# A conditioned transformer block on one core: layer-norm statistics shared between two engines, turned tokens kept by half, and some instructions moved in their queues

## The chip, the core and the metric

The kernel runs on one core of a Trainium2 chip. The core has TensorE (PE in the profile, with its weight loads listed apart as PEld), VectorE (DVE), ScalarE (ACT), GpSimd (POOL) and SyncE (SP), which issues most DMAs. Each engine works through its own queue in the order in which the program was written; engines wait for one another by semaphores. Matmuls write to PSUM, the small memory of banks beside the large on-chip SBUF.

The metric is device time in microseconds. A time given for a kernel is the median of its runs; the profile is of one execution, whose own time is given beside it.

## The reference, cut to what matters

```python
emb = jnp.dot(jax.nn.silu(t), ada_w) + ada_b            # adaLN, six parts of 512
shift_msa, scale_msa, gate_msa, shift_mlp, scale_mlp, gate_mlp = jnp.split(emb, 6, axis=-1)
norm = _ln(x) * (1.0 + scale_msa[:, None]) + shift_msa[:, None]
h = jax.nn.gelu(jnp.dot(norm, ssm_w1) + ssm_b1, approximate=False)
x = x + gate_msa[:, None] * (jnp.dot(h, ssm_w2) + ssm_b2)
norm2 = _ln(x) * (1.0 + scale_mlp[:, None]) + shift_mlp[:, None]
hf = jax.nn.gelu(jnp.dot(norm2, ff_w1) + ff_b1, approximate=True)
x = x + gate_mlp[:, None] * (jnp.dot(hf, ff_w2) + ff_b2)
```

x is 2 x 2048 x 512 in fp32 and t is 2 x 512. `_ln` subtracts the mean over the 512 features and divides by the root of the variance plus 1e-6. The weights are 512 x 3072 (ada_w), 512 x 512 (ssm_w1, ssm_w2), 512 x 1024 (ff_w1) and 1024 x 512 (ff_w2), all fp32.

## The kernel before

The 4096 tokens are cut into 8 blocks of 512. A block lies in SBUF as 128 partitions x 4 slots (c = 0 to 3) x 512 features. A block passes through: statistics (mean and variance of each token, `mv`), root (`ve`, and `r` by a power on GpSimd), a few tiny VectorE steps to `rstd` and `nmr`, `normal(c)` on ScalarE, a turn of tokens against features, the modulation by adaLN's shift and scale, the layer `hA` (W1 and GELU), the layer `oA` (W2, residual), a second norm, and the layers `hC` and `oC` of the feed-forward part.

All matrix products are made by fast recursive schemes: a product is split into quarters, and seven half-size products (P1 to P7) are made of sums of quarters in place of eight. So beside the matmuls there are sums of operands: of weights (`w1_sums`, `fw1_sums`, on GpSimd at L386), of tokens (`summed`, also recorded at L386, on VectorE or GpSimd) and of hidden values (`hSA`). `hidden` and `residual` issue the products of one layer in the order given (`FIRST` is P1, P2, P5, P6, P7, P3, P4; block 0's first layer runs P1, P2, P5, P6, P3, P7, P4). After each product VectorE reads its PSUM bank, ScalarE applies GELU where it is due, and then the hooks of that product run.

The order of all other work is written out by hand: `hook(hooks, ("P2",), ops)` puts operations behind product P2 of the layer that follows, in the order of the calls. An operation lands in the queue of its own engine, behind what was issued for it before. So a place in the hooks is a place in a queue.

What the change touches:

- **Statistics.** `stats()` runs a batch-norm statistic and an aggregate per slot on VectorE (L569, L570). `sums_on_act()` makes the four means on ScalarE with an accumulating activation (L581), `squares_on_act()` a negated mean `less` (L597) and four accumulated squares (L592). Their products lie in `unread`, which nobody reads and which has the one buffer `blocks` that the turned tokens use as well. Block 0's first norm uses `stats()`. Block 1's first norm and block 0's second norm use ScalarE for all four slots.
- **Root and gate rows.** `root` (L611, L612) needs the variances of all slots. `gate_rows_of(2)` makes 16 small matmuls on ada's third column block (`rows_of`, L287), and VectorE adds the bias row (L341). `first_ssm_gate` (L348) spreads these rows over the partitions by matmul; W2 is then folded with the gate on VectorE (L434). `rows_of(3)` and `rows_of(4)` (L287 too) take the fourth and fifth column blocks of ada_w.
- **Prologue.** Block 0's normalized tokens are turned by TensorE into four PSUM tiles, one for each feature group k (L702), each with all four slots. `modulate` reads them by half h (slots 0 and 1, then 2 and 3), k even on ScalarE (L723) and k odd on VectorE (L725), into `nT`; P1 of block 0's first layer needs half 0 of k = 0 and 1. `warm(1)` is a matmul on the identity whose result nobody reads (L1267).
- **Block 1's tokens.** They are turned by VectorE in 32 x 32 squares, one `turn(c)` for each slot (L686), then moved by 16 DMAs, half of them issued by SP and half by ScalarE (`move`, L695), then modulated in place (L723, L725). `later_loads` puts three more loads behind them on SP.

The initial loads all stand in SP's queue, in this order: x block 0, ada column blocks 0 and 1 in three pieces, ssm_w1 in two, x block 1, ada block 2, its bias rows, ssm_w2, ssm_b2, ada blocks 3 and 4, ff_w1.

Of the kernel before, what the change touches and what calls it, by code (L numbers as in the profile page):

```python
# [36 lines left out]
F32 = mybir.dt.float32  # L37
AF = mybir.ActivationFunctionType
# [102 lines left out]
def kernel(  # L141
# [16 lines left out]
    nc = tc.nc  # L158
    P = 128
    B, N, D = x.shape  # L160
# [3 lines left out]
    C = 4  # L164
    TB = C * P
# [7 lines left out]
    sums = ctx.enter_context(tc.tile_pool(name="sums", bufs=3))  # L173
    work = ctx.enter_context(tc.tile_pool(name="work", bufs=1))
    small = ctx.enter_context(tc.tile_pool(name="small", bufs=3))
    dram = ctx.enter_context(tc.tile_pool(name="dram", bufs=1, space=bass.MemoryType.DRAM))
    ps_t = ctx.enter_context(tc.tile_pool(name="ps_t", bufs=2, space=bass.MemoryType.PSUM))
    ps_g = ctx.enter_context(tc.tile_pool(name="ps_g", bufs=2, space=bass.MemoryType.PSUM))
# [18 lines left out]
    xs = {}  # L197
# [140 lines left out]
    def gate_rows_of(g):  # L338
        pa = rows_of(g)
        r = w2_t[:, 2 * P : 3 * P] if g == 2 else w2_t[:, 3 * P : 4 * P]  # L340
        nc.vector.tensor_tensor(r, pa[:, :P], gate_b[g], ALU.add)  # L341
        gate_rows[g] = r
# [207 lines left out]
    def hook(hooks, places, ops):  # L550

        for n, op in enumerate(ops):
            hooks.setdefault(places[min(n, len(places) - 1)], []).append(op)


    class Norm:
# [3 lines left out]
            self.i, self.which, self.name = i, which, f"{which}_{i}"  # L560
            self.xn, self.of_squares = {}, 1.0

        def stats(self):
            n = self.name
            self.mv = small.tile([P, C, nc.vector.BN_AGGR_DIM], F32, tag="mv", name=f"mv{n}")

            def op(c):
                st = small.tile([P, nc.vector.BN_STATS_DIM], F32, tag="st", name=f"st{n}_{c}")
                nc.vector.bn_stats(st, xs[self.i][:, c, :])  # L569
                nc.vector.bn_aggr(self.mv[:, c, :], st)  # L570

            return [lambda c=c: op(c) for c in range(C)]

        def sums_on_act(self):

# [8 lines left out]

            return [lambda c=c: op(c) for c in range(C)]

        def squares_on_act(self):

            less = small.tile([P, C], F32, tag="less", name=f"less{self.name}", bufs=1)

            def op(c):
                nc.scalar.activation(  # L592
                    self.unread[:, c], xs[self.i][:, c, :], AF.Square, bias=less[:, c : c + 1], accum_out=self.mv[:, c, 1:]
                )

            self.of_squares = 1.0 / D
            return [lambda: nc.scalar.activation(less, self.mv[:, :, 0], AF.Identity, scale=-1.0)] + [  # L597
                lambda c=c: op(c) for c in range(C)
            ]

        def scales(self):
# [98 lines left out]
        def transpose(self, c, pts, first):  # L700
            for k in range(KD):
                nc.tensor.matmul(  # L702
                    pts[k][:, c * P : (c + 1) * P],
                    self.xn[:, c, k * P : (k + 1) * P],
                    ident,
                    start=first,
                    stop=True,
                    is_transpose=True,
                    skip_group_check=True,
                )  # L710

        def modulate(self, k, pt=None, eng=None, h=None):
            b = self.i // PER_B
            g0 = 0 if self.which == 1 else 3
            shift, scale = [mods[g0, part][:, k, b : b + 1] for part in range(2)]
            if pt is None:
                dst = src = self.nT[:, :, k * P : (k + 1) * P]
            else:
                part = slice(h * C // 2, (h + 1) * C // 2)
                dst = self.nT.rearrange("p a (k c q) -> p a k c q", k=KD, c=C)[:, :, k, part]  # L720
                src = pt.rearrange("p (c a q) -> p a c q", c=C, a=C)[:, :, part]
            if eng is None:
                nc.scalar.activation(dst, src, AF.Identity, bias=shift, scale=scale)  # L723
            else:
                eng.tensor_scalar(dst, src, scale, shift, ALU.mult, ALU.add)  # L725
# [517 lines left out]
    def run(ops):  # L1243
        for op in ops:
            op()
# [4 lines left out]
    n1 = {0: Norm(0, 1), 1: Norm(1, 1)}  # L1250
# [9 lines left out]
    pt = ps_t.tile([P, 512], F32, tag="t", name="rowsT")  # L1260
# [4 lines left out]
    def warm(count, blocks=2):  # L1265
        for _ in range(count):
            nc.tensor.matmul(  # L1267
                idle[:, :blocks],
                ident,
                ident.unsqueeze(1).to_broadcast([P, blocks, P]),  # L1270
                start=True,
                stop=True,
            )
# [18 lines left out]
    w1_ops, w1_sums, _ = weight_of_first("w1", w1_sb)  # L1292
    run(w1_sums)
    pada_01 = ps_t.tile([P, D], F32, tag="t", name="pada_01")
    rows_01(pada_01, (0, 1))
    warm(1)
    for c in range(C):
        n1[0].normal(c, nc.vector if c % 2 else None, on_pe=True)
    for g in (1, 4):
        rows_g = colsT[:, R_ADA + g * KD : R_ADA + (g + 1) * KD]  # L1300
        nc.vector.tensor_scalar(rows_g, rows_g, 1.0, None, ALU.add)
    pts = [ps_g.tile([P, TB], F32, tag=t, name=f"pt1_0_{k}") for k, t in enumerate("yvxv")]
    rows_01(pada_01, (2,))
    n1[0].transpose(1, pts, True)
    rows_01(pada_01, (3,))
    for c in (0, 3, 2):
        n1[0].transpose(c, pts, False)
    modulation_01(pada_01)
    for h in range(2):
        for k in range(KD):  # L1310
            n1[0].modulate(k, pts[k], nc.vector if k % 2 else None, h)
    picks = brows[:, 3].rearrange("p (m q) -> p m q", m=P // G)
    nc.gpsimd.tensor_copy(
        picks, ident.rearrange("p (m q) -> p m q", q=G)[:, :, :1].to_broadcast([P, P // G, P])
# [1 line left out]
    n1_sums = n1[0].summed(nc.vector)  # L1316
# [12 lines left out]
    def fold2(lo, hi):  # L1329
        return [lambda k=k: found["w2"][1][k]() for k in range(lo, hi)]  # L1330

    hooks = {}
    hook(hooks, ("P1",), n1_sums[2:3])
    hook(hooks, ("P2",), n1_sums[3:])
    hook(hooks, ("P1",), n1[1].sums_on_act() + n1[1].squares_on_act())
    hook(hooks, ("P5",), [n1[1].root])
    hook(hooks, ("P6",), [lambda: gate_rows_of(2)])
    hook(hooks, ("P6",), [n1[1].rest] + [lambda c=c: n1[1].normal(c) for c in range(2)])
    hook(hooks, ("P3",), [ssm_gate] + [lambda: n1[1].turn(0)] + [lambda c=c: n1[1].normal(c) for c in range(2, 4)])
    hook(hooks, ("P7",), [gb2_0, lambda: seed("oA_0", b2_bc, 0), lambda: apart_row(b2_bc, nc.gpsimd)] + fold2(0, 4))  # L1340
    hook(hooks, ("P7",), fold2(4, 7) + [lambda: seed("oA_0", b2_bc, 1), lambda: found.update(pada=rows_of(3))])

# [6 lines left out]
    w2_ops = found["w2"][0]  # L1349

    hA_sums = hA[0].summed(nc.vector, nc.gpsimd)
    run([hA_sums[0], lambda: n1[1].turn(1), hA_sums[1], lambda: n1[1].turn(2), lambda: n1[1].turn(3)])
    run([lambda: n1[1].move((nc.sync, nc.scalar)), later_loads])
    hooks = {}
    hook(hooks, ("P1",), fold2(7, 8) + hA_sums[2:])
    hook(hooks, ("P2",), [lambda: modulation(3, 0, found["pada"])])
    hook(hooks, ("P6",), [lambda: found.update(pada=rows_of(4))])
# [2 lines left out]
    n2 = {0: Norm(0, 2)}  # L1360
# [13 lines left out]


    n1_sums = n1[1].summed(nc.vector)
    st = n2[0].sums_on_act() + n2[0].squares_on_act()
    hook(hooks, ("P3",), n1_sums[:2] + st[:2])
    residual("oA_0", 0, hA[0], w2_ops, KD // 2, hooks, order=FIRST)
    run(st[2:])  # L1380
    hooks = {}
    hook(hooks, ("P1",), n1_sums[2:3])
    hook(hooks, ("P2",), n1_sums[3:] + [n2[0].root])
    hook(hooks, ("P6",), [n2[0].rest] + [lambda c=c: n2[0].normal(c) for c in range(C)])
    hook(hooks, ("P5", "P7"), [lambda p=p: seed("oA_1", gb[2], p) for p in range(2)])
    hook(hooks, ("P5", "P7"), fw1_sums[1:3])
# [9 lines left out]
    hA_sums = hA[1].summed(nc.vector)  # L1396
    run(hA_sums[:2])
    n1[2] = Norm(2, 1)
    st = n1[2].stats()
    hooks = {}  # L1400
# [14 lines left out]
    hooks = {}  # L1415
# [25 lines left out]
    hooks = {}  # L1441
# [10 lines left out]
    hooks = {}  # L1452
# [7 lines left out]
    hooks = {}  # L1460
# [255 lines left out]
```

## Time and profile before

| | |
|---|---|
| time, median of 3 runs | 584.24 us (583.8 to 584.43) |
| the profiled execution's own time | 584.29 us |
| its span, first to last instruction | 582.5 us |
| mean granted TensorE clock | 1.000 |
| read from HBM / written to it | 32.8 MB / 8.4 MB |
| first stretch, 0 to 26 us: PE busy | 22.95 us |
| last stretch, 574 to 582.5 us: PE busy | 4.30 us |

How to read the rows below. The timeline gives start and length in microseconds, engine, source line, operation, the tile written and those read, the shapes, and in square brackets the idle time of the engine before the instruction and what ended it. "x8" means that eight like instructions follow one another in the row. One fp32 matmul of the program shows as two instructions. The chain of waits goes back from the last instruction to what released each step, and is printed in order of time. A table by stretches gives, for each, its length and then the busy time and number of instructions of PE, PEld, DVE, ACT and POOL, the granted clock, the DMA engines' busy share and GB/s. A row of the table of waits reads: who waited for whom, total, times, longest.

### The profile page before, as it was taken

The page shows a single profiled execution, that of the slowest core. Times are in us where ns is not written, and L with a number is a line of the kernel's source. Part 1 is how long each engine was busy: PE and PEld are TensorE (multiplying, and loading weights), DVE is VectorE, ACT ScalarE, POOL GpSimd, SP SyncE. Part 2 cuts the span into 40 slices and gives each one's busy share as a digit, 9 for nine tenths or more (in the row PEclk, how much of TensorE's full clock was granted, in tenths as well). Part 3 has the DMA queues.
Part 4 walks back from the last instruction along what each step waited for, and adds up shares of the span by engine and source line. Part 5 has one row for each costly group of instructions (what it writes and reads, how often), then busy time and mean ns, then how long its engine had stood idle before and what let it go on. Part 6 is the DMA issues. An engine that isn't in the chain of part 4 may idle for free.

```text
span 582.5 us, 9821 instructions
## 1 busy us (share of the span) xinstructions
PE 575.2 (99%) x3355; PEld 513.4 (88%) x3355; DVE 442.5 (76%) x892; ACT 284.9 (49%) x549; POOL 417.0 (72%) x447
## 2 busy tenths in 40 slices
PE   8999999999999999999999999999999999999997
PEld 4788888888889889998899988998898998899896
DVE  4777798996868576797867678986756487887677
ACT  2727357805642655535734588335664331732520
POOL 1574449999949788599968999997770593369351
PEclk9999999999999999999999999999999999999999
DMA  8967433303205303354033920243130330031002
GB/s 331 389 186 271 104 70 86 105 37 109 54 20 145 141 5 68 113 162 128 2 92 72 308 74 22 51 117 133 43 73 0 100 120 1 1 74 74 0 1 73
DMA packets 25534, 57.57 MB, mean 99 GB/s; under 512 B 4960, under 2 KB 6028, under 8 KB 23820
## 3 DMA queue, kind: packets, MB, share of 16 engines
q1 hardware_dynamic: 21760, 52.20, 28.5%
q10 hardware_dynamic: 3724, 4.75, 3.4%
q8 instruction: 27, 0.44, 0.3%
q14 instruction: 23, 0.19, 0.1%
HBM read 32.80 MB, written 8.40 MB: 71 GB/s over the span
## 4 chain that ended last, share of the span: by engine, by line
PE 93%; DMA 3%; DVE 2%; ACT 1%; issue 1%; ACTq 0%; SPq 0%; DVEq 0%
PE px_hC L1174 10%; PE py_hA L532 9%; PE py_hC L1174 8%; PE py_oC L944 8%; PE pv_hC L1174 8%; PE pl_oC_P_y L992 8%; PE py_oA L532 5%; PE pl_oC_P_v L992 5%; PE pv_hA L532 4%; PE py_oA L879 4%; PE pl_oC_P_x L992 3%; PE py_hC L532 2%; PE pv_oA L532 2%; PE py_oC L532 2%; PE px_hA L532 2%; DMA x<-in_x_dram 2%
## 5 line engine op out<-in xcount | busy, mean ns | idle before, releaser
L612 POOL TENSOR_TENSOR r<-ve,minus_half 128x4 f32<-128x4 f32 x16 | 16.5, 1033 | 71.7 <-DVE pl_oC_P_v L652 33.5
L723 ACT ACTIVATE nT<-nT,mod,mod 128x512 f32<-128x512 f32 x32 | 23.4, 803 | 56.0 <-DMA nT<-blocks 32.7
L1098 POOL TENSOR_TENSOR forms<-forms 128x256 f32<-128x256 f32 x56 | 41.9, 747 | 4.8 <-DVE forms L1094 1.3
L1174 PE MATMUL py_hC<-forms,fw 128*128 128x256 f32 x168 | 41.0, 380 | 0.0
L386 POOL TENSOR_TENSOR hSC<-hClo,hChi 128x512 f32<-128x512 f32 (+1 forms) x16 | 19.6, 1228 | 25.5 <-ACT hChi L1169 22.6
L1191 DVE TENSOR_TENSOR hClo<-hClo,py_hC 128x512 f32<-128x512 f32 x42 | 28.5, 684 | 11.6 <-ACT hClo L1188 8.5
L569 DVE BATCH_NORM_STATS2 st<-x 128x6 f32<-128x512 f32 x48 | 32.4, 675 | 4.8 <-DMA x<-in_x_dram 4.8
L1174 PEld LDWEIGHTS py_hC<-forms,fw 128*128 128x128 f32 x168 | 31.7, 190 | 4.8 <-DVE hClo L1191 0.5
L723 ACT ACTIVATE x<-x,mod 128x512 f32<-128x512 f32 x24 | 17.6, 802 | 34.9 <-DMA x<-blocks 25.8
L675 ACT ACTIVATE nT<-x,nmr,rstd 128x512 f32<-128x512 f32 x36 | 26.7, 804 | 6.4 <-DVE nmr L660 3.8
L686 DVE STREAM_TRANSPOSE blocks<-nT 128x512 f32<-128x512 f32 x36 | 25.0, 704 | 5.9 <-ACT nT L675 5.9
L1191 DVE TENSOR_TENSOR hChi<-hChi,pv_hC 128x512 f32<-128x512 f32 x35 | 23.2, 680 | 7.9 <-PE pv_hC L1174 6.7
L1169 ACT ACTIVATE hClo<-hClo,colsT 128x256 f32<-128x256 f32 x56 | 25.3, 498 | 5.4 <-DVE hClo L1191 5.3
L1174 PE MATMUL px_hC<-forms,fw 128*128 128x256 f32 x112 | 27.6, 379 | 0.0
L1188 ACT ACTIVATE hClo<-px_hC 128x512 f32<-128x512 f32 x21 | 12.5, 596 | 27.7 <-PE px_hC L1174 22.2
L1006 DVE TENSOR_TENSOR x<-pl_oC_P_y,x 128x256 f32<-128x256 f32 (+1 forms) x66 | 24.6, 374 | 1.9 <-PE pl_oC_P_y L992 0.6
L1169 ACT ACTIVATE hChi<-hChi,colsT 128x256 f32<-128x256 f32 x56 | 25.1, 495 | 1.9 <-DVE hChi L1191 1.9
L944 PE MATMUL py_oC<-fw_s,hSC 128*128 128x256 f32 x112 | 25.3, 379 | 0.0
L944 PE MATMUL py_oC<-fw,hClo 128*128 128x256 f32 x112 | 25.3, 379 | 0.0
L386 POOL TENSOR_TENSOR hClo<-hClo 128x512 f32<-128x512 f32 (+1 forms) x23 | 24.9, 1085 | 0.0
L1188 ACT ACTIVATE hChi<-py_hC 128x512 f32<-128x512 f32 x14 | 7.6, 595 | 33.4 <-PE py_hC L1174 24.8
L1174 PEld LDWEIGHTS px_hC<-forms,fw 128*128 128x128 f32 x112 | 21.3, 190 | 2.9
(414 smaller groups left out, 1851.6 us busy)
## 6 DMA issues: line engine op xcount, KB each, us to landing
x<-in_x_dram SPq DMA_DIRECT2D x13, 1024.0 KB
out_dram<-x SPq DMA_DIRECT2D x14, 512.0 KB
x<-blocks SPq DMA_DIRECT2D x96, 64.0 KB
nT<-blocks SPq DMA_DIRECT2D x88, 64.0 KB
ada<-in_L_cond_ada_w_dram SPq DMA_DIRECT2D x5, 1024.0 KB
fw<-in_L_cond_ff_w_dram SPq DMA_DIRECT2D x2, 2048.0 KB
nT<-blocks ACTq DMA_DIRECT2D x56, 64.0 KB
w<-in_L_cond_ssm_w_dram SPq DMA_DIRECT2D x2, 1024.0 KB
```

The lines of the kernel that those rows point to most:

```text
L386: eng.tensor_tensor(out[:, r], a[:, r], b[:, r], f)
L532: nc.tensor.matmul(ps[b][j * apart][:, j, :], lhs(p, j, k), rhs(p, j, k), start=(fresh and j * (not apart) == 0 and k == 0), stop=(p in (" ...
L569: nc.vector.bn_stats(st, xs[self.i][:, c, :])
L675: nc.scalar.activation(t, x_c, AF.Identity, bias=self.nmr[:, c : c + 1], scale=self.rstd[:, c : c + 1])
L686: nc.vector.transpose(self.bl[:, :, :, c, :].rearrange("p m k q -> p k m q"), self.nT[:, c, :].rearrange("p (k m q) -> p k m q", k=KD, m=C),)
L723: nc.scalar.activation(dst, src, AF.Identity, bias=shift, scale=scale)
L944: yield lambda j=j, k=k: nc.tensor.matmul(ps[BANK[p]][:, j, :], hops(p, j, k), wops[p][:, k, :], start=False, stop=(k == kdim - 1), skip_g ...
L992: nc.tensor.matmul(t[:, n, :], hops.leaves[p][f][:, k, :], leaf_wops[p][f][:, k, :], start=room not in started, stop=(f in ("P2", "P3", "P ...
L1098: eng.tensor_tensor(reg[d], reg[a], reg[b], ALU.add if f == "+" else ALU.subtract)
L1169: nc.scalar.activation(h, h, AF.Gelu_apprx_tanh, bias=fb1T[:, m : m + 1])
L1174: nc.tensor.matmul(ps[b][:, j, :], fa[ra][:, j * P : (j + 1) * P], fb[rb].rearrange("p a (c q) -> p c a q", q=Q), start=(fresh and j == 0) ...
L1191: nc.vector.tensor_tensor(dest(d), dest(d), ps[b], op)
```

## The change

It has four parts.

1. In the prologue, `warm(1)` between two groups of adaLN matmuls is left out, and block 0's turned tokens lie in four PSUM tiles by half h and parity of k, in place of four by k. Each tile holds two k of two slots, in the same four banks as before.
2. `mixed_stats` makes the statistics of slots 0 to 2 on ScalarE (three sums, `less`, three squares, scaled so that the accumulated value is the variance) and of slot 3 on VectorE. Block 1's first norm uses it: ScalarE's part stays behind P1 of block 0's first layer, VectorE's part stands behind P2, where the fourth token sum (`n1_sums[3:]`) stood. `root` moves from behind P5 to behind P6, ahead of the gate rows, and the fourth token sum follows these.
3. Block 1's `normal(2)` and `normal(3)` on ScalarE move from behind P3 of block 0's first layer to the end of that layer. `turn(2)`, `turn(3)`, the 16 DMAs and the later loads move behind P1 of the next layer (`oA_0`), and so behind VectorE's read of that product.
4. Block 0's second norm uses `mixed_stats` as well; VectorE's part stands behind P2 of block 1's first layer, ahead of `root`.

```diff
--- before.py
+++ after.py
@@ -560,9 +560,9 @@
             self.i, self.which, self.name = i, which, f"{which}_{i}"
             self.xn, self.of_squares = {}, 1.0
 
-        def stats(self):
+        def stats(self, mv=None):
             n = self.name
-            self.mv = small.tile([P, C, nc.vector.BN_AGGR_DIM], F32, tag="mv", name=f"mv{n}")
+            self.mv = mv or small.tile([P, C, nc.vector.BN_AGGR_DIM], F32, tag="mv", name=f"mv{n}")
 
             def op(c):
                 st = small.tile([P, nc.vector.BN_STATS_DIM], F32, tag="st", name=f"st{n}_{c}")
@@ -571,6 +571,11 @@
 
             return [lambda c=c: op(c) for c in range(C)]
 
+        def mixed_stats(self):
+
+            sums, var = self.sums_on_act(), self.squares_on_act(D**-0.5)
+            return sums[:3] + var[:4], self.stats(self.mv)[3:]
+
         def sums_on_act(self):
 
             n = self.name
@@ -584,18 +589,24 @@
 
             return [lambda c=c: op(c) for c in range(C)]
 
-        def squares_on_act(self):
+        def squares_on_act(self, scale=1.0):
 
             less = small.tile([P, C], F32, tag="less", name=f"less{self.name}", bufs=1)
+            n = C if scale == 1.0 else C - 1
 
             def op(c):
                 nc.scalar.activation(
-                    self.unread[:, c], xs[self.i][:, c, :], AF.Square, bias=less[:, c : c + 1], accum_out=self.mv[:, c, 1:]
+                    self.unread[:, c],
+                    xs[self.i][:, c, :],
+                    AF.Square,
+                    bias=less[:, c : c + 1],
+                    scale=scale,
+                    accum_out=self.mv[:, c, 1:],
                 )
 
-            self.of_squares = 1.0 / D
-            return [lambda: nc.scalar.activation(less, self.mv[:, :, 0], AF.Identity, scale=-1.0)] + [
-                lambda c=c: op(c) for c in range(C)
+            self.of_squares = 1.0 / D / scale**2
+            return [lambda: nc.scalar.activation(less[:, :n], self.mv[:, :n, 0], AF.Identity, scale=-scale)] + [
+                lambda c=c: op(c) for c in range(n)
             ]
 
         def scales(self):
@@ -700,10 +711,10 @@
         def transpose(self, c, pts, first):
             for k in range(KD):
                 nc.tensor.matmul(
-                    pts[k][:, c * P : (c + 1) * P],
+                    pts[c // 2, k % 2][:, k // 2, c % 2],
                     self.xn[:, c, k * P : (k + 1) * P],
                     ident,
-                    start=first,
+                    start=(first and k < 2),
                     stop=True,
                     is_transpose=True,
                     skip_group_check=True,
@@ -718,7 +729,7 @@
             else:
                 part = slice(h * C // 2, (h + 1) * C // 2)
                 dst = self.nT.rearrange("p a (k c q) -> p a k c q", k=KD, c=C)[:, :, k, part]
-                src = pt.rearrange("p (c a q) -> p a c q", c=C, a=C)[:, :, part]
+                src = pt[h, k % 2][:, k // 2].rearrange("p c (a q) -> p a c q", a=C)
             if eng is None:
                 nc.scalar.activation(dst, src, AF.Identity, bias=shift, scale=scale)
             else:
@@ -1293,22 +1304,24 @@
     run(w1_sums)
     pada_01 = ps_t.tile([P, D], F32, tag="t", name="pada_01")
     rows_01(pada_01, (0, 1))
-    warm(1)
     for c in range(C):
         n1[0].normal(c, nc.vector if c % 2 else None, on_pe=True)
     for g in (1, 4):
         rows_g = colsT[:, R_ADA + g * KD : R_ADA + (g + 1) * KD]
         nc.vector.tensor_scalar(rows_g, rows_g, 1.0, None, ALU.add)
-    pts = [ps_g.tile([P, TB], F32, tag=t, name=f"pt1_0_{k}") for k, t in enumerate("yvxv")]
+    pts = {
+        (h, g): ps_g.tile([P, 2, 2, P], F32, tag=t, name=f"pt1_0_{h}_{g}")
+        for (h, g), t in zip(((0, 0), (0, 1), (1, 0), (1, 1)), "yvxv")
+    }
     rows_01(pada_01, (2,))
     n1[0].transpose(1, pts, True)
     rows_01(pada_01, (3,))
     for c in (0, 3, 2):
-        n1[0].transpose(c, pts, False)
+        n1[0].transpose(c, pts, c == 3)
     modulation_01(pada_01)
     for h in range(2):
         for k in range(KD):
-            n1[0].modulate(k, pts[k], nc.vector if k % 2 else None, h)
+            n1[0].modulate(k, pts, nc.vector if k % 2 else None, h)
     picks = brows[:, 3].rearrange("p (m q) -> p m q", m=P // G)
     nc.gpsimd.tensor_copy(
         picks, ident.rearrange("p (m q) -> p m q", q=G)[:, :, :1].to_broadcast([P, P // G, P])
@@ -1331,12 +1344,12 @@
 
     hooks = {}
     hook(hooks, ("P1",), n1_sums[2:3])
-    hook(hooks, ("P2",), n1_sums[3:])
-    hook(hooks, ("P1",), n1[1].sums_on_act() + n1[1].squares_on_act())
-    hook(hooks, ("P5",), [n1[1].root])
-    hook(hooks, ("P6",), [lambda: gate_rows_of(2)])
+    on_act, on_dve = n1[1].mixed_stats()
+    hook(hooks, ("P1",), on_act)
+    hook(hooks, ("P2",), on_dve)
+    hook(hooks, ("P6",), [n1[1].root, lambda: gate_rows_of(2)] + n1_sums[3:])
     hook(hooks, ("P6",), [n1[1].rest] + [lambda c=c: n1[1].normal(c) for c in range(2)])
-    hook(hooks, ("P3",), [ssm_gate] + [lambda: n1[1].turn(0)] + [lambda c=c: n1[1].normal(c) for c in range(2, 4)])
+    hook(hooks, ("P3",), [ssm_gate, lambda: n1[1].turn(0)])
     hook(hooks, ("P7",), [gb2_0, lambda: seed("oA_0", b2_bc, 0), lambda: apart_row(b2_bc, nc.gpsimd)] + fold2(0, 4))
     hook(hooks, ("P7",), fold2(4, 7) + [lambda: seed("oA_0", b2_bc, 1), lambda: found.update(pada=rows_of(3))])
 
@@ -1349,9 +1362,11 @@
     w2_ops = found["w2"][0]
 
     hA_sums = hA[0].summed(nc.vector, nc.gpsimd)
-    run([hA_sums[0], lambda: n1[1].turn(1), hA_sums[1], lambda: n1[1].turn(2), lambda: n1[1].turn(3)])
-    run([lambda: n1[1].move((nc.sync, nc.scalar)), later_loads])
+    n1[1].normal(2)
+    n1[1].normal(3)
+    run([hA_sums[0], lambda: n1[1].turn(1), hA_sums[1]])
     hooks = {}
+    hook(hooks, ("P1",), [lambda: n1[1].turn(2), lambda: n1[1].turn(3), lambda: n1[1].move((nc.sync, nc.scalar)), later_loads])
     hook(hooks, ("P1",), fold2(7, 8) + hA_sums[2:])
     hook(hooks, ("P2",), [lambda: modulation(3, 0, found["pada"])])
     hook(hooks, ("P6",), [lambda: found.update(pada=rows_of(4))])
@@ -1374,13 +1389,13 @@
 
 
     n1_sums = n1[1].summed(nc.vector)
-    st = n2[0].sums_on_act() + n2[0].squares_on_act()
+    st, on_dve = n2[0].mixed_stats()
     hook(hooks, ("P3",), n1_sums[:2] + st[:2])
     residual("oA_0", 0, hA[0], w2_ops, KD // 2, hooks, order=FIRST)
     run(st[2:])
     hooks = {}
     hook(hooks, ("P1",), n1_sums[2:3])
-    hook(hooks, ("P2",), n1_sums[3:] + [n2[0].root])
+    hook(hooks, ("P2",), n1_sums[3:] + on_dve + [n2[0].root])
     hook(hooks, ("P6",), [n2[0].rest] + [lambda c=c: n2[0].normal(c) for c in range(C)])
     hook(hooks, ("P5", "P7"), [lambda p=p: seed("oA_1", gb[2], p) for p in range(2)])
     hook(hooks, ("P5", "P7"), fw1_sums[1:3])
```

## The prediction

> **What bounds the kernel now.** I read the page's busy shares first, then its chain that ended last.
>
> ```profile
> span 582.5 us, 9821 instructions
> PE 575.2 (99%) x3355; PEld 513.4 (88%) x3355; DVE 442.5 (76%) x892; ACT 284.9 (49%) x549; POOL 417.0 (72%) x447
> ...
> PE 93%; DMA 3%; DVE 2%; ACT 1%; issue 1%; ACTq 0%; SPq 0%; DVEq 0%
> ```
>
> TensorE is the chain for 93% of the span. Busy time by stretches shows where it is not:
>
> ```profile
> 26.00:82.00 56.00, 56.00 (x338) 46.99 (x337) 45.43 (x90) 29.95 (x57) 27.44 (x25) 1.00 0.58 177
> 82.00:574.00 492.00, 492.00 (x2815) 446.94 (x2814) 377.26 (x754) 242.02 (x464) 378.83 (x405) 1.00 0.26 76
> ```
>
> PE (the first figure after the length) is never idle from 26 us to 574. All edits work before 74 us; what they save there moves the rest forward, if no later wait takes it. The chain in order of time shows what comes before PE:
>
> ```profile
> 6.21 12.03 DMA x<-in_x_dram
> ...
> 18.34 2.57 ACT unread L581 x8
> ...
> 20.94 0.21 ACT less L597
> ...
> 21.80 2.31 ACT unread L592 x7
> ...
> 24.14 0.07 DVE ve L611
> ...
> 24.82 0.28 DVE w_t L341
> ```
>
> Block 1 lands at 18.24; ScalarE makes four sums and four squares of it until 24.11; VectorE's root (L611) waits for them, and the gate rows (L341) stand behind the root in VectorE's queue. In the timeline PE's weight loads mark best who waits, since a load follows the one before without a gap unless something is late:
>
> ```profile
> 21.45 0.81 PEld L287 LDWEIGHTS pada<-ada,w_t 128*32 128x32 f32 x32 [0.33 <-ACT less L597]
> ...
> 22.46 1.59 PEld L532 LDWEIGHTS pv_hA<-nT,w_s 128*128 128x128 f32 x8 [0.20 <-issue]
> ...
> 25.21 0.97 PEld L348 LDWEIGHTS pgate<-w_t,fw_t 128*128 128x128 f32 x8 [1.16 <-issue]
> ...
> 26.10 1.60 PEld L532 LDWEIGHTS py_hA<-nT,w 128*128 128x128 f32 x8
> ...
> 28.03 0.81 PEld L287 LDWEIGHTS pada<-ada,w_t 128*32 128x32 f32 x32 [0.33 <-issue]
> ...
> 30.82 1.16 PEld L532 LDWEIGHTS py_oA<-w,forms 128*128 128x128 f32 x6 [0.18 <-ACT py_oA L504]
> ```
>
> The 0.33 before the 32-column loads and the 0.20 behind them recur without a cause and stay. The 1.16 before the gate (L348) is the stall: the gate rows were done at 25.10.
>
> **Part 1: turned tokens by half, and no warm(1).**
>
> ```profile
> 10.13 0.70 PE L1267 MATMUL idle<-w_t 128*128 128x256 f32 x2
> ...
> 13.13 0.17 DVE L321 TENSOR_TENSOR mod<-pada,colsT 128x16 f32<-128x16 f32 x1
> ...
> 13.73 1.93 ACT L723 ACTIVATE nT<-pt,mod 128x256 f32<-128x256 f32 x4 [1.94 <-PE pt L702]
> ...
> 14.35 1.59 PEld L532 LDWEIGHTS py_hA<-nT,w 128*128 128x128 f32 x8 [0.57 <-ACT nT L723]
> ```
>
> The modulation was ready at 13.30 (13.13 + 0.17), but ScalarE began at 13.73, after the last token group had been turned into the same tile. With a tile for each half it begins at about 13.36: 0.37 earlier. Without the 0.70 us of idle matmul the adaLN products stand earlier too, by at most 0.70; their weights are still landing then, so I take 0.2. P1 then starts at about 13.8 instead of 14.35, 0.55 earlier. Bounds: 0 to 1.07.
>
> **Part 2: block 1's statistics, and the root after P6.** ScalarE loses one sum (2.57 / 4 = 0.64) and one square:
>
> ```profile
> 21.90 0.71 ACT L592 ACTIVATE unread<-x,less 128x512 f32<-128x512 f32 x1
> ...
> 24.22 0.68 DVE L787 TENSOR_TENSOR forms<-py_hA,colsT 128x512 f32<-128x512 f32 x1
> ```
>
> It ends at 24.11 - 0.64 - 0.71 = 22.8. VectorE gains one statistic and one aggregate:
>
> ```profile
> 5.58 0.66 DVE L569 BATCH_NORM_STATS2 st<-x 128x6 f32<-128x512 f32 x1
> ...
> 6.28 0.18 DVE L570 BATCH_NORM_AGGREGATE mv<-st 128x2 f32<-128x6 f32 x1
> ```
>
> That is 0.84, in the place of the fourth token sum, which moves behind the gate rows. Queued behind it are the reads of P5 and P6 (L787, 0.68 each), which now precede the root; P6's product ends near 21, so both are done by 22.1. Root 22.8 to 23.0, gate rows 0.28, ready at 23.3. The moved sum follows and ends by 24.5; only P4, past 28, wants it.
>
> On PE the 0.55 of part 1 reaches the gate's own rows (the load at 21.45) only as far as their weights have landed. SP's next issue of that line waited for just this landing:
>
> ```profile
> SPq L209 <- DMA ada<-in_L_cond_ada_w_dram: 2.3, 1, 2.3
> ...
> 20.98 0.37 SPq L209 DMA_DIRECT2D ada<-in_L_cond_ada_w_dram  x1
> ...
> ada<-in_L_cond_ada_w_dram SPq DMA_DIRECT2D x5, 1024.0 KB
> ...
> w<-in_L_cond_ssm_w_dram SPq DMA_DIRECT2D x2, 1024.0 KB
> ...
> gb<-in_L_cond_ssm_b_dram SPq DMA_DIRECT2D x2, 256.0 KB
> ```
>
> So these rows start at about 21.07, gain 0.38. P3's load starts at 21.07 + 0.81 + 0.20 = 22.08 and ends at 23.67, after the gate rows; the gate follows at 23.87 instead of 25.21: gain 1.34. P7 is 1.34 earlier too, and the rows behind it (28.03) could start at 26.69. They need the fourth adaLN block. One megabyte took 20.97 - 18.24 = 2.73; behind it come w2 (1 MB), b2 (0.25) and this block (1): 2.25 x 2.73 = 6.1, so it lands at an estimated 27.1. **The gain is cut to 28.03 - 27.17 = 0.86.** Without part 1 PE would be there at about 27.1 as well: part 1 adds next to nothing to part 2, and a DMA cuts part 2. Bounds: 0.5 (a landing 0.36 later) to 1.34 (no cut).
>
> ScalarE now has normals 2 and 3 behind all activations of block 0's first layer, so its seeds come earlier and the 0.18 at 30.82 goes: 0.1 above what recurs.
>
> **Part 3: turns 2 and 3 behind the first read.**
>
> ```profile
> 33.08 1.13 DVE L386 TENSOR_TENSOR hSA<-hSA,forms 128x512 f32<-128x512 f32 x1
> ...
> 34.13 1.29 DVE L686 STREAM_TRANSPOSE blocks<-nT 128x512 f32<-128x512 f32 x2
> ...
> 35.35 0.65 DVE L842 TENSOR_TENSOR x<-py_oA,x 128x512 f32<-128x512 f32 x1
> ...
> 36.11 1.59 PEld L532 LDWEIGHTS py_oA<-w_s,hSA 128*128 128x128 f32 x8 [0.25 <-issue]
> ...
> 42.77 1.52 ACT L723 ACTIVATE nT<-nT,mod 128x512 f32<-128x512 f32 x2 [10.72 <-DMA fw_t<-in_L_cond_ada_b_dram]
> ...
> 44.12 1.70 PEld L532 LDWEIGHTS py_hA<-nT,w 128*128 128x128 f32 x8
> ```
>
> The read that P6 (36.11) waited for no longer stands behind two turns: 0.2, which makes 0.86 + 0.1 + 0.2 = 1.16. In exchange the turns, and the 16 DMAs and the later loads behind them in the queues of SP and ScalarE, come after that read (0.65). VectorE's queue there hangs on P7, 1.34 earlier, so the last turn ends at 35.42 - 1.34 + 0.65 = 34.73, 0.69 earlier. The first modulated piece was there at 42.77 + 0.76 = 43.53; now at 42.84, and PE arrives at 44.12 - 1.16 = 42.96. Cost 0, with 0.12 to spare.
>
> **Part 4: block 0's second statistics.**
>
> ```profile
> 51.00 0.17 DVE L611 TENSOR_SCALAR ve<-mv 128x4 f32<-128x4 f32 x1 [1.73 <-ACT unread L592]
> ...
> 61.18 0.94 PEld L532 LDWEIGHTS py_oA<-w_s,hSA 128*128 128x128 f32 x5 [0.27 <-DVE x L842]
> ...
> 66.56 1.59 PEld L532 LDWEIGHTS pv_oA<-w,hSA 128*128 128x128 f32 x8 [0.33 <-DVE x L842]
> ...
> 73.69 1.59 PEld L532 LDWEIGHTS py_hC<-nS,fw_s 128*128 128x128 f32 x8 [0.36 <-issue]
> ```
>
> VectorE's 0.84 fits into the 1.73 in which it only waited, and ScalarE is done 1.35 sooner. So the root and what follows come some 0.4 to 0.9 earlier against PE, which shortens the late reads behind PE's three small stalls (0.96 together): between 0 and 0.9; I take 0.25, since VectorE is busy for most of that stretch.
>
> **Sum:** 1.16 + 0.25 = 1.4. The profiled execution took 584.29 (582.5 and 1.8 around it; the median of the runs is 584.24), so **582.9**.
>
> [...] PE's clock stands at 1.00 in both stretches above. [...] No row here shows a drop, not even beside the 1.16 without a load at 25.
>
> **Rivals.**
> - *Only the first, cut gain stays*, 0.86 + 0.1: each small stall returns behind a full VectorE. For: 45.43 busy of 56. Against: all its reads come earlier. 583.3.
> - *More*: the fourth block does not bind and all stalls go: 1.34 + 0.1 + 0.2 + 0.9 = 2.5, so 581.8.
> - *Slower, by the move*: turns 2 and 3 end late, because VectorE beside GpSimd takes 1.13 for an operation instead of 0.68. PE's arrival at 44.12 before left 0.5 behind a last turn at 35.42; past 35.9 PE starts later than before, one for one. Six operations at 0.45 more are 2.7: 34.73 + 2.7 = 37.4, 1.5 past the point, 585.8. Against: the turns and the read took 0.65 each beside GpSimd.
> - *It doesn't do what it says*: the aggregate writes into the tile that ScalarE is filling and is held until 22.8. The two L787, root and rows follow (0.2 + 1.2 + 0.2 + 0.3): rows at 24.7; P3 wants the first of those reads (23.6) and delays the gate to 25.45, 0.24 later than before: 584.5. Against: P1 started when the first of eight modulated pieces of nT stood, so waits on such a tile go by region.
> [...]
>
> **Chances.** Forecast 0.48, its own range 582.4 to 583.4; first gain only 0.20; more 0.10; slower by the move 0.12; held aggregate 0.06; clock 0.04. About 0.2% (1.2 us) is what a measurement of this kernel tells from no change. Faster, under 583.1: 0.40 of the forecast, 0.10 of "more", 0.04 of the second, 0.54. Slower, over 585.4: 0.06, 0.03 and 0.02 of the last three, 0.11. The same: 0.35. The range 582.0 to 584.7 leaves out most of the move and of the clock, and the far end of "more".
>
> **What would show it.** The gate's load at 23.9 behind a gap of 0.2; the rows after P7 at about 27.1, behind a gap above 0.33; the root at 22.8; the DMAs of L695 from 34.8; no gap at the first read's product (36.11 before) and none at block 1's first product (44.12). The forecast is wrong if that product starts behind a gap put down to L723, if the clock falls under 1.00 before 20 us, or if the three stalls after 60 grow.

## The result, and the profile after

The changed kernel took 582.85 us (median of 11 runs, 582.48 to 583.78) beside 584.21 for the kernel before on the same chip (583.47 to 585.1). The ratio is 0.9981, with a 95% interval of 0.9972 to 0.999: 1.36 us saved, 0.6 to 1.6 by the interval. The profiled execution of the changed kernel is the slowest of its eleven, 583.78 us, so the two profiled executions differ by only 0.51 us, and their rows can't add up to the 1.36 of the medians.

The page of the changed kernel:

```profile
span 582.0 us, 9813 instructions
...
PE 574.1 (99%) x3353; PEld 513.5 (88%) x3353; DVE 444.0 (76%) x896; ACT 282.6 (49%) x541; POOL 416.7 (72%) x447
```

Two of the 3355 matmul instructions are gone, the idle matmul, and eight of ScalarE's: two sums and two squares, each counted twice. Now the chain in order of time (start, length, engine), and then the timeline. Lines moved: L723 is L734, L592 is L598, L581 is L586, L611 is L622, L695 is L706, L842 is L853.

```profile
5.93 10.95 DMA x<-in_x_dram
...
16.89 10.82 DMA ada<-in_L_cond_ada_w_dram
...
27.85 1.08 PE pada L287 x32
```

```profile
13.80 1.59 PEld L532 LDWEIGHTS py_hA<-nT,w 128*128 128x128 f32 x8 [0.23 <-ACT nT L734]
...
16.98 0.63 ACT L586 ACTIVATE unread<-x 128x512 f32<-128x512 f32 x1 [1.86 <-DMA x<-in_x_dram]
...
20.90 0.18 DVE L570 BATCH_NORM_AGGREGATE mv<-st 128x2 f32<-128x6 f32 x1
...
21.17 0.84 PEld L287 LDWEIGHTS pada<-ada,w_t 128*32 128x32 f32 x32 [0.59 <-issue]
...
21.23 0.19 ACT L598 ACTIVATION_READ_ACCUMULATOR unread<-x,less 128x1 f32 x1
...
21.57 0.68 DVE L798 TENSOR_TENSOR forms<-py_hA,colsT 128x512 f32<-128x512 f32 x1
...
22.17 0.16 DVE L622 TENSOR_SCALAR ve<-mv 128x4 f32<-128x4 f32 x1
...
22.34 0.29 DVE L341 TENSOR_TENSOR w_t<-pada,fw_t 128x128 f32<-128x128 f32 x1
...
23.83 1.08 PEld L348 LDWEIGHTS pgate<-w_t,fw_t 128*128 128x128 f32 x8
...
27.82 0.84 PEld L287 LDWEIGHTS pada<-ada,w_t 128*32 128x32 f32 x32 [1.40 <-PE py_hA L532]
...
34.81 5.44 SPq L706 DMA_DIRECT2D nT<-blocks  x8
...
35.66 1.70 PEld L532 LDWEIGHTS py_oA<-w_s,hSA 128*128 128x128 f32 x8
...
41.99 1.52 ACT L734 ACTIVATE nT<-nT,mod 128x512 f32<-128x512 f32 x2 [8.86 <-DMA fw_t<-in_L_cond_ada_b_dram]
...
43.77 1.70 PEld L532 LDWEIGHTS py_hA<-nT,w 128*128 128x128 f32 x8
...
65.86 1.59 PEld L532 LDWEIGHTS pv_oA<-w,hSA 128*128 128x128 f32 x8 [0.19 <-DVE x L853]
...
76.42 1.59 PEld L532 LDWEIGHTS py_hC<-nT,fw 128*128 128x128 f32 x8 [0.33 <-issue]
```

The gate's load has no bracket: the stall of 1.16 is gone, and PE is there 1.38 earlier. At the rows behind P7 a gap of 1.40 stands, with the name of a PE instruction in it. PE had nothing to wait for from itself; the chain names the true releaser, the fourth adaLN block, landed at 16.89 + 10.82 = 27.71. That leaves 0.21 of the 1.38. More is won back by the gaps that are gone at 30.8, 36, 61 and 73: at 76.42 PE is 0.88 earlier (77.30 before).

One row was not foreseen at all: the first sum starts at 16.98. Its line before was 18.34, and nothing in the change touches the load of block 1. By stretches (length; busy us of PE, PEld, DVE, ACT, POOL; clock), the start and the stretch after it:

```profile
9.00:12.00 3.00, 2.60 (x64) 1.92 (x68) 1.81 (x8) 1.52 (x2) 0.46 (x1) 1.00 1.02 408
12.00:15.50 3.50, 3.50 (x36) 2.90 (x25) 2.94 (x7) 1.93 (x4) 1.02 (x1) 1.00 1.05 417
...
26.00:82.00 56.00, 54.97 (x334) 46.92 (x333) 45.33 (x88) 27.25 (x50) 27.46 (x25) 1.00 0.59 181
```

The clock stays at 1.00 without the idle matmul. PE lacks 1.03 us of the third stretch, nearly all of it the wait for the fourth block.

### The profile page after: what moved, and what is told of

Read it like the earlier page. It is cut to its first block, busy times and chain, and to the rows that moved or that the text cites. A ratio compares the mean times of both kernels' runs of the same rounds, so it can differ in the third digit from the quotient of the medians.

```text
span 582.0 us, 9813 instructions
## 1 busy us (share of the span) xinstructions
PE 574.1 (99%) x3353; PEld 513.5 (88%) x3353; DVE 444.0 (76%) x896; ACT 282.6 (49%) x541; POOL 416.7 (72%) x447
## 4 chain that ended last, share of the span: by engine, by line
PE 92%; DMA 4%; DVE 2%; issue 0%; ACTq 0%; SPq 0%; DVEq 0%
PE px_hC L1185 10%; PE py_hA L532 9%; PE py_hC L1185 8%; PE py_oC L955 8%; PE pv_hC L1185 8%; PE pl_oC_P_y L1003 8%; PE py_oA L532 5%; PE pl_oC_P_v L1003 5%; PE pv_hA L532 4%; PE py_oA L890 4%; PE pl_oC_P_x L1003 3%; PE py_hC L532 2%; PE pv_oA L532 2%; PE py_oC L532 2%; PE px_hA L532 2%; PE pv_oC L1003 2%
## 5 line engine op out<-in xcount | busy, mean ns | idle before, releaser
L623 POOL TENSOR_TENSOR r<-ve,minus_half 128x4 f32<-128x4 f32 x16 | 16.5, 1033 | 70.1 <-DVE ve L622 28.9
L734 ACT ACTIVATE nT<-nT,mod,mod 128x512 f32<-128x512 f32 x32 | 23.4, 803 | 56.3 <-DMA nT<-blocks 33.2
L569 DVE BATCH_NORM_STATS2 st<-x 128x6 f32<-128x512 f32 x50 | 33.8, 677 | 4.8 <-DMA x<-in_x_dram 4.8
L734 ACT ACTIVATE x<-x,mod 128x512 f32<-128x512 f32 x24 | 17.6, 803 | 35.4 <-DMA x<-blocks 26.2
```

## The experiments

There were twelve runs: ten kernels, and a second profile each of the kernel before and of part 1 alone. "Theory" and "rival" are those of the text ahead of each.

### Part 1 alone

To the kernel before: part 1 of the change (tiles by half, no idle matmul), with parts 2 to 4 left out. The prediction had said that it adds next to nothing.

> The kernel before with the turned tokens by half and without warm(1), nothing else. Theory: P1 starts at 13.8 instead of 14.35, PE then waits longer ahead of the gate (a gap of some 1.5 instead of 1.16), the gate stays at 25.2, time 584.2, between 583.9 and 584.4. Rival: the 0.55 gained at P1 is kept, 583.7.

Measured: 583.05 us, ratio 0.9982 (0.9974 to 0.9991). Theory and rival both fell: part 1 alone is worth 1.2 us, almost as much as the whole change. Its timeline shows how:

```profile
17.48 0.63 ACT L581 ACTIVATE unread<-x 128x512 f32<-128x512 f32 x1 [1.76 <-DMA x<-in_x_dram]
...
24.35 0.97 PEld L348 LDWEIGHTS pgate<-w_t,fw_t 128*128 128x128 f32 x8 [0.20 <-issue]
```

Four sums and squares stand on ScalarE as before, but they start 0.86 earlier, because block 1 landed earlier; the gate is 0.86 earlier too.

### The root moved, alone

```diff
-    hook(hooks, ("P5",), [n1[1].root])
-    hook(hooks, ("P6",), [lambda: gate_rows_of(2)])
+    hook(hooks, ("P6",), [n1[1].root, lambda: gate_rows_of(2)])
```

> The kernel before with the root moved from behind P5 to behind P6, ahead of the gate rows; all statistics still on ScalarE. Theory: the two reads of P5 and P6 no longer stand behind the root's wait, so the gate rows are ready 0.17 + 0.28 after ScalarE's end (24.1), at 24.6 instead of 25.10: the gate starts 0.5 earlier, time 583.7. Rival (only the shared statistic pays): 584.2.

Measured: 583.6 us, 0.9993 (0.9984 to 1.0002), near the theory's 583.7, but the interval does not tell it from no change. From its timeline:

```profile
18.55 0.63 ACT L581 ACTIVATE unread<-x 128x512 f32<-128x512 f32 x1 [2.78 <-DMA x<-in_x_dram]
...
24.95 0.97 PEld L348 LDWEIGHTS pgate<-w_t,fw_t 128*128 128x128 f32 x8 [0.80 <-issue]
```

The gate is 0.26 earlier than before, though block 1 landed 0.21 later in this execution. Counted from the first sum, the gate comes after 6.40 in place of 6.87 (25.21 - 18.34): the root's place is worth 0.47 of the stall of 1.16, about the 0.5 of the theory. The 0.80 that is left goes with the statistics, as the kernel without part 1 shows below.

### What moved block 1's landing

The DMA engines are full with loads at that time (shares of 1.02 and 1.05 in the stretches above, and 1.02 from 14 to 20 us in the kernel before). The table of DMA queues (packets, MB, time of the packets as a share of 16 engines) in 0.1 us from 15.9 of the kernel before, and from 16.6 of the changed one, has a queue of another kind:

```profile
q8 instruction: 1, 0.02, 67.9%
```

```profile
q8 instruction: 1, 0.02, 68.7%
```

One packet of 16 KB, which took 0.679 x 16 x 0.1 = 1.09 us on one of the 16 engines. The page of the kernel before counts 27 of them, 0.44 MB together:

```profile
q8 instruction: 27, 0.44, 0.3%
```

No view tells whose instructions these packets hold; that they are PE's, as the texts ahead of the runs have it, is my guess. PE did not wait while this one moved (busy 1.20 us of the 1.20 from 15.9 to 17.1), but a load may have. Theory F: the idle matmul sets when this packet falls, and at 15.9 it falls into the last of block 1. By the shares above the loads keep all 16 engines busy, so I take it that block 1 is spread over them and complete only with its slowest piece; no view shows it engine by engine. Four runs: the kernel before and part 1 alone profiled a second time, and part 1 taken apart, first without the idle matmul alone.

```diff
-    warm(1)
```

The second kernel has the other half of part 1, and `warm(1)` stays:

```diff
-                    pts[k][:, c * P : (c + 1) * P],
+                    pts[c // 2, k % 2][:, k // 2, c % 2],
...
-            n1[0].modulate(k, pts[k], nc.vector if k % 2 else None, h)
+            n1[0].modulate(k, pts, nc.vector if k % 2 else None, h)
```

> The kernel before once more, for a second profile. Theory F (a late landing sets the stall): in the first profile a 16 KB packet of the instruction queue started at 15.93, while block 1 was landing, and block 1 was complete at 18.24; here again such a packet between 15 and 17, ScalarE's first sum after 18.1 and a gap over 1 us ahead of the gate. Rival (the packet falls anywhere, from one execution to the next): it is found past 20, block 1 is complete by 17 and the gap is under 0.5.

> The kernel before with the first part alone once more, for a second profile. Theory F: the packet falls after block 1's last bytes again (after 16.5), ScalarE's first sum starts by 17.5 and the gap ahead of the gate is under 0.6. Rival (chance): a packet at 16 or before, a first sum after 18.1 and a gap over 1.3, as PE comes 0.55 earlier.

> The kernel before without warm(1), nothing else. Theory F: four PE instructions fewer shift the fetch of PE's next instructions past block 1's landing, so this edit alone makes what part 1 made: 583.1 (582.8 to 583.4). Rival (PE's earlier P1 made it): P1 is at most 0.2 earlier here, 584.0 (583.8 to 584.3).

> The kernel before with the turned tokens by half, warm(1) kept. Theory F: the number of PE instructions is that of before, the fetch falls into block 1's landing again, the gate stays where it was: 584.2 (583.9 to 584.5). Rival (PE's earlier P1 made it): P1 is 0.35 to 0.4 earlier, 583.5 (583.2 to 583.8).

Measured: without the idle matmul 582.99 us, 0.9982 (0.9973 to 0.9991); with the tiles by half alone 584.16, 0.9997 (0.9988 to 1.0006). The two repeats took 584.39 and 582.85 in one execution each. Now first sum and gate in the timeline, first of the two that have the idle matmul, the kernel before again and the tiles alone:

```profile
18.38 0.63 ACT L581 ACTIVATE unread<-x 128x512 f32<-128x512 f32 x1 [2.63 <-DMA x<-in_x_dram]
...
25.25 0.97 PEld L348 LDWEIGHTS pgate<-w_t,fw_t 128*128 128x128 f32 x8 [1.11 <-issue]
```

```profile
18.37 0.63 ACT L581 ACTIVATE unread<-x 128x512 f32<-128x512 f32 x1 [2.79 <-DMA x<-in_x_dram]
...
25.25 0.97 PEld L348 LDWEIGHTS pgate<-w_t,fw_t 128*128 128x128 f32 x8 [1.27 <-issue]
```

And the kernel before without the idle matmul:

```profile
17.10 0.63 ACT L581 ACTIVATE unread<-x 128x512 f32<-128x512 f32 x1 [1.52 <-DMA x<-in_x_dram]
...
24.00 1.08 PEld L348 LDWEIGHTS pgate<-w_t,fw_t 128*128 128x128 f32 x8
...
27.69 0.79 PEld L287 LDWEIGHTS pada<-ada,w_t 128*32 128x32 f32 x29 [1.10 <-PE py_hA L532]
...
65.73 1.59 PEld L532 LDWEIGHTS pv_oA<-w,hSA 128*128 128x128 f32 x8 [0.18 <-DVE x L842]
...
76.26 1.59 PEld L532 LDWEIGHTS py_hC<-nT,fw 128*128 128x128 f32 x8 [0.30 <-issue]
```

One matmul less, whose result nobody read, and the whole stall at the gate is gone with the statistics untouched. P1 isn't what did it: its load starts at 14.27 here, and at 14.27 with the tiles alone too, where nothing is gained. (With the tiles alone the gap ahead of P1 falls from 0.57 to 0.22, but the adaLN products stood 0.27 later in that execution; so the rival's P1, 0.35 to 0.4 earlier, did not come about.)

SP's issues tell how long a load took: one of them waits for ssm_w1 (at about 13), one for block 1 and one for ada's third block. Counted from one to the next, over all profiles of this study:

| | instruction packet starts | block 1 after ssm_w1 | ada's third block after block 1 | first sum of block 1 starts |
|---|---|---|---|---|
| with the idle matmul, 6 profiles | 15.9 to 16.3 | 5.05 to 5.40 | 2.53 to 2.73 | 18.20 to 18.55 |
| without it, 4 profiles | 16.5 to 16.8 | 3.84 to 3.85 | 3.90 to 4.19 | 16.85 to 17.12 |
| without it, 4 profiles | 23.4 to 24.1 | 3.84 to 3.85 | 2.71 to 2.77 | 17.01 to 17.48 |

A packet at 16.6 comes when little of block 1 is left, and meets the next load, ada's third block. SP's next issue of that line waits for its landing; in the changed kernel, whose packet came at 16.6, and in the one without the idle matmul, whose packet came at 24:

```profile
21.08 0.37 SPq L209 DMA_DIRECT2D ada<-in_L_cond_ada_w_dram  x1
```

```profile
19.73 0.37 SPq L209 DMA_DIRECT2D ada<-in_L_cond_ada_w_dram  x1
```

Block 1 at 18.24 against 16.88, this block at 21.08 against 19.73: about 1.35 each time. By the table the load that a packet meets takes 1.1 to 1.7 longer than the same load without one, in all 14 profiles; that is somewhat more than the packet's own 1.09. Part 1 alone shows both cases in one and the same kernel: with the packet at 23.85 the third block took 2.77, and in the second profile, with the packet at 16.80, it took 4.00. So the matmul itself is not needed for such a delay, only the packet's place.

I could not move the packet on purpose: that it is the cause rests on this agreement of place and size. Why one matmul moves it by 0.7 or 8 us stays open, and so does why it moves by 7 us between two executions of one kernel. Where it fell in the executions without a profile is not known: the kernel before has some of 583.3 to 583.5, and part 1 alone has one of 584.8 among its eleven.

### The change without part 1

To the changed kernel: part 1 undone, parts 2 to 4 stay.

> The changed kernel with the first part undone (warm(1) back, turned tokens by feature group). Theory: the fetch falls into block 1's landing again, ScalarE's first sum starts at about 18.3, but with three slots and the root behind P6 the gate rows are ready by 23.4, no gap over 0.3 ahead of the gate; PE then waits for the fourth column block at 27.1 as before: 583.1 (582.8 to 583.4). Rival (all of the gain is warm(1)): 584.2.

Measured: 583.06 us, 0.9985 (0.9976 to 0.9994), as the theory had it. Its timeline:

```profile
18.25 0.63 ACT L586 ACTIVATE unread<-x 128x512 f32<-128x512 f32 x1 [2.54 <-DMA x<-in_x_dram]
...
22.73 0.17 DVE L622 TENSOR_SCALAR ve<-mv 128x4 f32<-128x4 f32 x1 [0.39 <-ACT unread L598]
...
24.14 1.08 PEld L348 LDWEIGHTS pgate<-w_t,fw_t 128*128 128x128 f32 x8
...
27.06 0.81 PEld L287 LDWEIGHTS pada<-ada,w_t 128*32 128x32 f32 x32 [0.33 <-issue]
...
43.20 1.59 PEld L532 LDWEIGHTS py_hA<-nT,w 128*128 128x128 f32 x8 [0.24 <-ACT nT L734]
```

Block 1 is late again, and the root comes at 22.73, as it was forecast for such a landing (22.8). Part 2 (shared statistics and the root's place) takes the gate's stall away without part 1. So the idle matmul and part 2 each remove the same 1.16; 1.2 and 1.1 together make 1.36, not 2.3. At 43.20 block 1's first product waits for its first modulated piece: the move in part 3 has this cost, which the changed kernel does not show, since PE comes later there. None of the kernels without part 3 has a gap at that product.

### The fourth adaLN block, earlier and later

Does its landing cut the gain? To the changed kernel, that block and ssm_w2 exchanged in SP's queue, with ssm_b2 between them as before:

```diff
-    w2_sb = load_w("w2", w2)
+    load_ada(3)
...
-    load_ada(3)
+    w2_sb = load_w("w2", w2)
```

> Theory (a landing cuts the gain): in the changed kernel the rows behind P7 stand behind a gap of 1.40 in the profiled execution and wait for adaLN's fourth column block. Loaded ahead of b2 and w2 the block is there by about 24.5, the gap falls to the recurring 0.33, and the rows start at 26.8. w2 then lands at about 27.7, shortly before its folds (28.1). Time 582.2, between 581.7 and 582.6, 0.3 to 1.1 under the changed kernel's 582.85. Rival (the landing costs nothing, a later stall takes the gain): 582.85, or slower where w2 comes too late for the folds.

And the other way, `load_ada(4)` ahead of `load_ada(3)`:

> The fourth column block is loaded behind the fifth, 1 MB later. Theory: it lands about 2.7 us later, PE waits for it one for one at the rows behind P7 (load at about 30), time 585.0 to 585.6. Rival: PE is not held there, 582.9.

Measured: earlier 582.52 us (582.43 to 582.58), 0.9971 (0.996 to 0.9982), the lowest median here, though its interval overlaps that of the changed kernel; later 587.24 (585.44 to 588.79), 1.0048 (1.0031 to 1.0065). The rows behind P7, earlier (with the stretch after 26) and later:

```profile
26.53 0.81 PEld L287 LDWEIGHTS pada<-ada,w_t 128*32 128x32 f32 x32 [0.33 <-issue]
...
42.64 1.59 PEld L532 LDWEIGHTS py_hA<-nT,w 128*128 128x128 f32 x8 [0.21 <-ACT nT L734]
...
26.00:82.00 56.00, 56.00 (x339) 47.68 (x338) 47.46 (x93) 29.16 (x54) 27.77 (x27) 1.00 0.58 182
```

```profile
29.57 0.84 PEld L287 LDWEIGHTS pada<-ada,w_t 128*32 128x32 f32 x32 [3.48 <-issue]
```

Earlier, the gap is the 0.33 that recurs, and PE's matmuls leave no idle time from 26 to 82. Later, the profiled execution took 585.44 with a mean clock of 1.000, and that is what 3.48 in place of 1.40 makes of 583.78 (585.9) less some 0.4. But four of the six executions took 587.2 to 588.8 with a mean clock of 0.993 to 0.996, and so the median misses the range expected. The clock lost is about the time lost: 0.004 to 0.007 of 587 us is 2.3 to 4.1, and the four took 1.8 to 3.4 us more than 585.44. What lowered their clock is not shown, since the four have no profile; the execution whose profile has the gap of 3.48 kept 1.000, as did the changed kernel's with its gap of 1.40.

### The order of loads on the other kernels

The kernel before with the fourth block earlier; the same without the idle matmul; and the changed kernel with the fourth block earlier, but parts 3 and 4 undone.

> The kernel before with the fourth column block loaded ahead of b2 and w2. Theory: the gate is released at 25.2 by block 1's statistics, the rows behind P7 come at 28.0, long after the landing in either order: 584.2 (583.9 to 584.5). Rival (an earlier block helps by itself): 583.8 or less.

> The kernel before without warm(1) and with the fourth column block loaded ahead of b2 and w2; no other part of the change. Theory: no gap over 0.35 ahead of the gate nor behind P7; what parts 2 to 4 save beyond that is only the small stalls at 30, 36 and after 60: 582.8 (582.5 to 583.0). Rival (parts 2 to 4 are needed as soon as the landing does not cap): 583.0 or more.

> The changed kernel with the fourth column block first, parts 3 and 4 undone. Theory: the small stalls at 36 (0.2) and after 60 (up to 0.3) come back: 582.9 (582.6 to 583.1) against 582.52 with them. Rival (parts 3 and 4 do nothing): 582.5.

Measured: 584.08, 0.9997 (0.9988 to 1.0006): nothing, since the gate's stall (0.91 here) still holds PE back. 583.15, 0.9984 (0.9975 to 0.9992): nothing beside the 582.99 with the old order, and here the rival was right. 582.75, 0.9978 (0.9969 to 0.9987). The timeline of the second, where PE reaches the rows 1.03 earlier than with the old order and loses it again in the small stalls:

```profile
26.66 0.81 PEld L287 LDWEIGHTS pada<-ada,w_t 128*32 128x32 f32 x32 [0.33 <-issue]
...
34.74 1.59 PEld L532 LDWEIGHTS py_oA<-w_s,hSA 128*128 128x128 f32 x8 [0.30 <-issue]
...
59.77 1.59 PEld L532 LDWEIGHTS py_oA<-w_s,hSA 128*128 128x128 f32 x8 [0.28 <-DVE x L842]
...
65.15 1.59 PEld L532 LDWEIGHTS pv_oA<-w,hSA 128*128 128x128 f32 x8 [0.33 <-DVE x L842]
...
72.30 1.59 PEld L532 LDWEIGHTS py_hC<-nS,fw_s 128*128 128x128 f32 x8 [0.38 <-issue]
```

In the third, without parts 3 and 4, PE waits 0.36 at 29.46, none at 34.6, and 0.24, 0.33 and 0.23 at the last three places; with them and this order one of 0.33 is left, and the new 0.21 at 42.64 comes in. The medians differ by only 0.23 and their intervals overlap, so the worth of parts 3 and 4 is seen in the trace rather than in the time. One more reason shows far behind the change. The timeline has the same product late in the changed kernel, in the one with the fourth block earlier, and in the one without part 1:

```profile
282.99 1.59 PEld L1185 LDWEIGHTS py_hC<-forms,fw 128*128 128x128 f32 x8 [0.36 <-DVE hClo L1202]
```

```profile
281.75 1.59 PEld L1185 LDWEIGHTS py_hC<-forms,fw 128*128 128x128 f32 x8 [0.37 <-DVE hClo L1202]
```

```profile
282.29 1.59 PEld L1185 LDWEIGHTS py_hC<-forms,fw 128*128 128x128 f32 x8 [0.36 <-DVE hClo L1202]
```

The one with that block later has the same 0.36 there. These four are the ones of the 14 profiles that have parts 3 and 4; none of the other ten waits at that product. So some 0.36 is given back 200 us later. How the parts cause it was not tried.

## Why the prediction was right, and where it was not

The time came out as forecast, 582.9 against 582.85, and the saving as the sum had it, 1.4 against 1.36. The steps behind it hold in part.

**Right: a stall at the gate, cut by a DMA.** The gate's load was put at 23.87 and came at 23.83; the adaLN rows behind P7 wait behind a gap above 0.33 that a load ends, and moving that load alone takes the gap to 0.33 or to 3.48. Its landing was an estimate, 27.1; it was 27.7 in the profiled execution, the slowest of its eleven, and the repeat of part 1 alone has the rows at 27.22. So the cut gain was 0.21 there where 0.86 was forecast. The order that lifts the cut agrees with the rival "more" in its mechanism, but with 0.3 us for it and not 1.1, by medians whose intervals overlap.

**Right in the signs, the cause not shown by them: parts 3 and 4.** The DMAs of the move came at 34.8, the gap before the product at 36 is gone, and at block 1's first product there is none: the first modulated piece stood at 41.99 + 0.76 = 42.75, and PE came at 43.77, 1.0 later where 0.12 had been forecast, since PE was late from the wait at 27.8. Of the three small stalls two are gone and one fell from 0.33 to 0.19. But this can't be put down to parts 3 and 4: the kernel before without the idle matmul, which waits 1.10 at the rows and has neither part, has lost the same gaps and keeps 0.18 at 65.73. I take it that the other engines catch up while PE waits there; this was not tried. The worth of parts 3 and 4 shows only where PE comes to the rows on time. With the fourth block earlier, with them and without, they take away 0.36 at 29.46, 0.24 at 59.61 and 0.23 at 71.99. The 0.2 that part 3 was to save at 36 is shown by no pair that differs in parts 3 and 4 alone. And where PE comes on time the 0.12 to spare at block 1's first product isn't there: the product waits 0.21 and, without part 1, 0.24 for its modulated piece. What no step had, too, is that 0.36 returns at 283; the bounds of the sum ended at 82 us.

**Wrong: the removed matmul counted only as PE time, at most 0.70 us.** P1's start came as forecast (13.80), but an earlier P1 is not what part 1 is worth: P1 stood at 14.27 with either half of it alone, and the tiles alone gain nothing (584.16). The idle matmul's removal is worth 1.2 us by another way, block 1 landing at 16.9 in place of 18.24. The working took that landing as fixed. So the root, forecast for 22.8, came at 22.17, held by then by VectorE's last read (21.57 + 0.68) and no longer by ScalarE, done at 21.42. The sentence that part 1 adds next to nothing to part 2 holds (582.85 with it, 583.06 without, where the rows behind P7 start at 27.06 as the working said); what the working missed is that part 1 alone does at the gate what part 2 does. The kernel without part 1 saves 1.1 (0.4 to 1.4) of the 1.4. That the whole change lands within 0.1 us of 582.9 is in part luck: in the one execution with a profile the terms come to 0.21 for the cut gain and some 0.67 for the small gaps, less 0.36 at 283, which is about the 0.51 between the two profiled executions and not 1.4. What the executions near the median did otherwise isn't known.

**The rivals.** The held aggregate fell: it runs at 20.90, while ScalarE writes squares into that tile until 21.42. The slower move fell, with 1.0 to spare in the changed kernel; where PE came on time it cost 0.2, not 1.5. A lower clock early in the kernel, to which a chance of 0.04 went (0.02 of it among the slower times), is shown by no run: from 9 to 15.5 us it stood at 1.00 in the changed kernel. "Only the first, cut gain" fell in its reason, since no small stall came back behind a full VectorE before 82 us.

## What to carry to other kernels

Two edits that remove the same stall don't add up (here 1.2 and 1.1 us, and 1.36 together): find the next thing that is late (here a load, four places back in a queue) before adding gains, and move that too; the load order was worth nothing on the kernel before, and 0.3 us on the changed one by medians whose intervals overlap. A gap that goes behind such a wait proves nothing for an edit made there: compare two kernels in which TensorE comes to the place at the same time. Where a kernel's start hangs on loads, an instruction that computes nothing can still cost more than its own duration (here 1.2 us for one of 0.70), so take such fillers out one at a time and look at when the loads land. A landing time of the kernel before is no constant (block 1 at 18.24 before, at 16.88 in the changed kernel): profile it twice, and after each edit compare it first.

## What the runs showed of the hardware

An instruction packet of 16 KB took 1.09 us on a DMA engine, and in all 14 profiles the 1 MB load that met it took 1.1 to 1.7 us longer than the same load in the profiles where none met it (block 1: 5.05 to 5.40 against 3.85 us; the third adaLN block: 3.90 to 4.19 against 2.53 to 2.77). And the kernel whose profile has a PE gap of 3.48 us ran with a mean clock of 0.993 to 0.996 in four of six executions and of 1.000 in two, which spread its times over 3.4 us, while the six executions of the kernel with the gap at 0.33 stay within 0.15.
